# A factorization-machine layer on one core: the product of the squares as eight block products of three passes each, and another order of the first products

## The chip, the core and the metric

The kernel runs on one core of one Trainium2 chip. The core's engines run side by side, each with its own queue of instructions: TensorE (PE; its weight loads are listed as PEld), VectorE (DVE), ScalarE (ACT), GpSimd (POOL), and SyncE (SP), which here only starts transfers. DMAs are started from the queues of SP, ACT and POOL; those of POOL can add what they bring to what lies at the destination. The metric is the device time of one execution in microseconds.

## The reference

x is 1024 x 512, weight 64 x 512 x 512 (e, f, m), lin_w 512 x 512, all float32:

```python
out_lin = x @ lin_w.T + lin_b
xv = jnp.einsum('bf,efm->bem', x, weight)
zp = jnp.einsum('bf,efm->bem', jnp.square(x), jnp.square(weight))
interaction = 0.5 * jnp.sum(jnp.square(xv) - zp, axis=1)
return out_lin + interaction
```

The sum over e of zp is one product, of x squared with the sum over e of weight squared. It is 512 x 512 x 1024, as large as the linear one; the 64 products of xv are the bulk.

## The kernel before

All products are made by one level of Strassen's scheme: X (A11, A12, A21, A22: halves of the batch by halves of f) and the other operand are cut in four blocks, and seven products of sums of blocks take the place of eight. Everything is transposed so that f lies on the partitions, 128 at a time, two tiles (KH = 2) to half of f.

There are three stages.

1. **The linear stage**: seven products (`one_level`, line 504), each 4 matmuls of plain float32, 128 x 128 by 512. A plain float32 matmul appears in the profile as two instructions. The result waits in DRAM (`lin_dram`).
2. **The main stage**: 32 groups h of 512 columns (8 columns m for all 64 e), each with the products 1, 6, 2, 3, 7, 5, 4 in that order (`ORDER`), where product 5 is made a group ahead. A product is two halves; a half is two 128-row tiles j, held by one of four double banks of PSUM (`banks`). Each operand is split into float32r parts H, L and K (`split` for weights, `x_pieces` for X, once), and a half is made by three passes: front (H and L, 8 matmul instructions in a half) and back (K, 4 in a half), where the back passes come later by `LAG` slots, and between the two the bank is scaled and added to (DVE, or ACT for product 5). The loads of w11, w12, w21, w22 land in rings of raw tiles; T is their running sum, made by adding DMAs (`load`, `load_more`): T = w11 + w12 for product 5, + w22 for 6, + w21 for 4. `split` makes H on ACT and L on POOL or DVE, and K on POOL. `finish` squares a finished bank on ACT into a ring of two tiles, and DVE sums over e into `acc`. `w_squares` squares a raw weight tile and sums over e into `w2_sum`. In group 0, products 1 and 2 (`PLAIN`) are plain float32. Product 5 of group 0 comes first of all.
3. **The last stage**, the product of the squares: X is loaded again and squared, Strassen's sums of the squares are made by adding DMAs (`add_square`), those of `w2_sum` on POOL (`column_sums`), and `one_level` makes the seven products, plain float32 again. Each half of a sum is added to the output tiles as it comes (`into`, 128 x 512), and these are stored. The output tiles hold the linear result from DRAM and, by an adding DMA, the accumulator (`acc_dram`, written by `turn`, which transposes 32 columns at a time). The last quarter of the accumulator's columns comes by a load of its own (`last`) and a DVE operation.

The order of all this is not written out. Each operation is entered with `plan.add` and its cost in us on the engines that can do it; `key` gives PE's order, and `Plan.order` lays out the others by due times in a list schedule over 60 rounds, which it improves where PE waited in its own reckoning. What it gives is a fixed order for each engine. Costs it reckons with are `PASS` = 0.2267 for a float32r matmul instruction and `WHOLE` = 0.858 for a plain matmul; a DMA takes 1.6 us of the wire (3.1 if it adds) and 2.5 us to land. `both=True` marks DVE operations that the planner keeps apart from POOL's.

Buffers go by rings, and many of the last stage's tiles lie in rings of the main stage: X's squares in raw tiles, output tiles in the tiles kept for products 1 and 5. `home` and `give_back` do the same for the linear stage's tiles at the start.

Names in the profile leave out numbers: `w` is any tile of the rings w11 to w22 or the kept tile w, `p` those kept for products 1 and 5 (and at the start what lies there), `sq` and `wsq` squares, `pH`, `pL`, `pK` the weight's parts, `X1H` to `X7K` X's parts. Lines of helpers: 360 ACT's, 366 and 372 DVE's two kinds, 378 POOL's, 385 the sums over e, 392 plain DMAs, 397 adding ones; 697 is the main stage's matmul, 522 that of `one_level`, 511 that of its first product.

Of the kernel before, what the change touches and what calls it, by code (L numbers as in the profile page):

```python
# [18 lines left out]
P = 128  # L19
# [3 lines left out]

PE, DVE, ACT, POOL, SP = "PE", "DVE", "ACT", "POOL", "SP"

PLAIN = (1, 2)
LAG = 4
ORDER = (1, 6, 2, 3, 7, 5, 4)
SPLIT = {**dict.fromkeys(range(1, 8), POOL), 2: DVE, 3: DVE}
MORE = True  # L30
X_SPLIT = {5: DVE, 6: DVE, 3: DVE, 7: DVE, 1: DVE, 2: "DMA", 4: "DMA"}
FIRST = dict.fromkeys(range(1, 8), POOL)
SCALE = {1: "DVE", 5: "ACT"}
RAW = {"w11": 2, "w12": 2, "w21": 1, "w22": 2, "T": 2}
PIECES = {"H": 3, "L": 3, "K": 3}
# [6 lines left out]
class Plan:  # L42
# [104 lines left out]
    def forward(self, chain):  # L147
# [62 lines left out]
        while len(done) < len(ops):  # L210
            now = heapq.heappop(times)
            moved = True
            while moved:
                moved = False
                for e in pending:
# [7 lines left out]
                        continue  # L223
                    moved = True
                    if e == PE:
                        nxt, mark = nxt + 1, running[PE]
                        late = max(late, now - o.latest)
                    cost = o.costs[e]
                    o.start, o.engine = now, e
# [27 lines left out]
def kernel(  # L257
# [118 lines left out]
    def pool(o, a, b, sub, reads, writes, size=1024):  # L376
        def emit(_):
            return (nc.gpsimd.tensor_sub if sub else nc.gpsimd.tensor_add)(o, a, b)  # L378

        plan.add({POOL: 0.1 + 2.24 * size / 1024}, emit, reads, writes)  # L380
# [14 lines left out]
    def dma_add(o, i, reads, writes, move=3.1, land=2.5):  # L395
        plan.add(
            {POOL: 0.62}, lambda _: nc.gpsimd.dma_start(o, i, accum_op=ALU.add),  # L397
            tuple(reads) + tuple(writes), writes, land=land, move=move,
        )

    def used(*names):
        plan.add({NONE: 0.0}, None, (), names)
# [98 lines left out]
    def four():  # L501
        return [both_of(banks()) for _ in range(4)]
# [101 lines left out]
    def src(h, q):  # L604
        return weight[h // NCB, q][:, h % NCB]

    def load(h, n, q):
        now[h, n] = raw[n]()
        dma(buf[now[h, n]], src(h, q), (), (now[h, n],))

    def load_more(h, n, q):

        o = now[h, n]
        if h or MORE:
            dma_add(buf[o], src(h, q), (), (o,))
        else:
            i = now[h, QUAD[q]]
            pool(buf[o], buf[o], buf[i], False, (o, i), (o,))

    def w_squares(h, q):  # L620
        row, col = divmod(QUAD.index(q), 2)
# [20 lines left out]

    def prepare(h, p):
        if p == 5:
            load(h, "T", 0)
            if h:
                load_more(h, "T", 1)
                load(h, "w11", 0)
            load(h, "w12", 1)
            if not h:  # L650
                load_more(h, "T", 1)
                load(h, "w11", 0)
                load(h, "w22", 3)
                load(h, "w21", 2)
            w_squares(h, "w12")
        if p == 1:
            if h:
                load(h, "w22", 3)
            w_squares(h, "w11")
        if p == 6:  # L660
            load_more(h, "T", 3)
            if h:
                load(h, "w21", 2)
            w_squares(h, "w22")
        if p == 2:
            w_squares(h, "w21")
        if p == 7:
            load_more(h, "w12", 3)
        if p == 4:
            load_more(h, "T", 2)  # L670
        n = now[h, RHS[p]]
        return n if not h and p in PLAIN else split(n, SPLIT[p] if h else FIRST[p])

# [95 lines left out]

    for g in range(NG):  # L770
        acc_name[g] = acc_ring()
    product(0, 5)
    for h in range(NH):
        for p in ORDER:
            if p != 5:
                product(h, p)
            elif h + 1 < NH:
                product(h + 1, p)
            if not h:
                give_back(*(n for n in ("A11", "A12", "A22") if OPERAND[p] == n))  # L780
        if h % NCB == NCB - 1 and h + 1 < NH:
            turn(h // NCB)
# [1 line left out]


    out_dst = out.rearrange("(c p) b -> p c b", p=P)
    sq_home = {}
    for n, q in (("A21", "T"), ("A22", "w11"), ("A11", "w22"), ("A12", "w12")):
        sq_home[n] = raw[q]()
    for n, q in (("R5", "w11"), ("R6", "w21"), ("R3", "w12")):  # L790
        sq_home[n] = raw[q]()
    sq_home["R7"] = sq_home["A21"]

    def load_square(n, again=None):
        r, q = quads[n]
        o = sq_home[n]
        dma(buf[o], x_src[:, ts(q, KH), ts(r, H)], (), (o,))
        if again:
            act(buf[sq_home[again]], buf[o], AF.Square, (o,), (sq_home[again],))
        act(buf[o], buf[o], AF.Square, (o,), (o,))  # L800

    def add_square(n, m):
        o, i = sq_home[n], sq_home[m]
        dma_add(buf[o], buf[i], (i,), (o,))

    def minus(n, m):
        o, i = sq_home[n], sq_home[m]
        act(buf[o], buf[i], AF.Copy, (i,), (o,), scale=-1.0)

    load_square("A21")  # L810
    minus("A21", "A21")
    load_square("A22", "R5")
    add_square("R5", "A21")
    load_square("A11", "R6")
    add_square("R6", "R5")
    add_square("R7", "A11")
    load_square("A12")
    minus("R3", "A12")
    add_square("R3", "R6")
    w2 = {(r, c): w2_sum[:, ts(r, KH), ts(c, HM)] for r in range(2) for c in range(2)}  # L820
    w2_names = {z: (("w2h", *z),) for z in w2}
    for (r, c), ap in w2.items():
        plan.add({ACT: 0.6}, lambda _, ap=ap: nc.scalar.mul(ap, ap, -0.5),
                 tuple(("w2", r, m) for m in range(M)
                       if ("w2", r, m) in plan.writer and m // HM == c), w2_names[r, c])
    wt_home = [raw[q]() for q in ("w22", "T")]
    wt = {
        k: buf[wt_home[(k - 1) // 2]][:, (k - 1) % 2].rearrange("p (k m) -> p k m", k=KH)
        for k in range(1, 5)
    }  # L830
    wt_names = {k: (("wt", k),) for k in range(1, 5)}
    for z, n in enumerate(wt_home):
        used(n, ("wt", 2 * z + 1), ("wt", 2 * z + 2))
    column_sums(w2, wt, w2_names, wt_names,
                lambda o, a, b, r, w: pool(o, a, b, False, r, w, 512))
    act(wt[2], wt[2], AF.Copy, wt_names[2], wt_names[2], 512, -1.0)
    left = {i: (buf[sq_home[n]], (sq_home[n],)) for i, n in OPERAND.items()}
    right = rhs_of(w2, w2_names, wt, wt_names)

    turn(NG - 1)  # L840
    o_name = {}

    def acc_names(ch):
        return tuple(("accd", g, q) for g in range(NG) for q in range(P // MG)
                     if g * MG // P == ch)

    for (r, c), n in (((0, 0), "p1"), ((1, 0), "p1"), ((1, 1), "p5"), ((0, 1), "p5")):
        n = o_name[r, c] = kept[n]()
        for u in range(2):
            used((n, u), n)  # L850
        dma(buf[n], lin_dram[:, ts(c, 2), ts(r, H)], (("lind", r, c),), both_of(n))
        for u in range(2):
            ch = 2 * c + u
            if ch < M // P - 1:
                dma_add(buf[n, u], acc_dram[:, ch, ts(r, H)], acc_names(ch), ((n, u),), 1.4, 5.0)

    def into(n, bank, sub, u):
        o = buf[n][:, u]
        dve(o, o, buf[bank[u]], sub, ((n, u), bank[u]), ((n, u),))

    def store(r, c, u):
        n = o_name[r, c]
        dma(out_dst[:, 2 * c + u, ts(r, H)], buf[n, u], ((n, u),), (), 1.0, (SP, ACT))

    def columns(n, m, sub, u):
        o, i = buf[n][:, u], buf[m][:, u]
        dve(o, o, i, sub, ((n, u), (m, u)), ((n, u),), 512, True)

    v, f2, f5, f4 = four()
    f3 = f4[0], f2[0]  # L870
    key = slot[0]
    one_level(1, right, left, v, True, key)
    one_level(2, right, left, f2, True, key + 4)
    for u in range(2):
        into(o_name[0, 0], v, False, u)
        into(o_name[0, 0], f2, False, u)
        store(0, 0, u)
    one_level(5, right, left, f5, True, key + 6)
    z = kept["w"]()
    for u in range(2):  # L880
        used((z, u), z)
        act(buf[z, u], buf[f5[u]], AF.Copy, (f5[u],), ((z, u),), 512)
        for r in range(2):
            columns(o_name[r, 1], z, True, u)
    one_level(6, right, left, v, False, key + 8)
    for u in range(2):
        into(o_name[0, 1], v, True, u)
    one_level(4, right, left, f5, True, key + 11)
    for u in range(2):
        into(o_name[1, 0], f5, False, u)  # L890
    last = wsquare()
    for r in range(2):
        used((last, r), last)
    for r in (1, 0):
        dma(buf[last][:, r], acc_dram[:, M // P - 1, ts(r, H)], acc_names(M // P - 1),
            ((last, r),), 1.0)
        n = o_name[r, 1]
        stt(buf[n, 1], buf[last][:, r], 0.5, buf[n, 1], ALU.add, ((last, r), (n, 1)), ((n, 1),),
            512, True)

    one_level(7, right, left, v, False, key + 14)
    for u in range(2):
        into(o_name[1, 1], v, True, u)
        store(1, 1, u)
        into(o_name[1, 0], v, False, u)
        store(1, 0, u)
    one_level(3, right, left, f3, True, key + 17)
    for u in range(2):
        into(o_name[0, 1], f3, True, u)
        store(0, 1, u)  # L910

    for op, engine in plan.order():
        if op.emit:
# [40 lines left out]
```

## Time and profile before

| | us |
|---|---|
| runs, median of 3 (lowest to highest) | 1285.91 (1285.85 to 1286.28) |
| the profiled execution, its own time | 1285.96 |
| its span, first to last instruction | 1284.0 |

The granted clock of TensorE was 0.999 of full speed over the span. HBM was read for 160.43 MB and written for 6.29 MB, 130 GB/s over the span.

How rows are read. A row of groups has: line, engine, operation, out<-in by names, shapes, xcount, then busy time, mean ns of one, and the idle time of the engine before them with what ended it. A row of the timeline has the start and the length in us, then the same, with idle time before it and its releaser in brackets. A row of waits has who waited for whom: us in total, times, longest. The chain that ended last has start, length and what. DMA rows have KB of one and the median us from issue to landing.

### The profile page before, as it was taken

The numbers are of one execution on the slowest core, as the hardware profiler recorded it, in microseconds if no ns is written. First come the engines' busy times: TensorE is split into PE (matmuls) and PEld (weight loads), VectorE is DVE, ScalarE is ACT, GpSimd is POOL, SyncE is SP. The second block draws the span as 40 slices with busy tenths as digits, with TensorE's granted clock in tenths as the row PEclk, the third lists the DMA queues.
The fourth block names the chain that finished last, engine by engine and source line by source line (L and its number), as shares of the span: only waits on it lengthen the run. The fifth ranks groups of instructions, "written<-read, shape, count | busy, mean of one in ns | idle before, by whom it ended". The sixth has DMA issues, their size and how long they took to land.

```text
span 1284.0 us, 15422 instructions
## 1 busy us (share of the span) xinstructions
PE 1277.9 (100%) x5476; PEld 1024.1 (80%) x5476; DVE 1224.3 (95%) x1018; ACT 963.9 (75%) x1005; POOL 1043.5 (81%) x532
## 2 busy tenths in 40 slices
PE   9999999999999999999999999999999999999998
PEld 4688888888888888888888888888888888888883
DVE  7799999999999999999999999999999999999996
ACT  6677877777787777877777878777778777787781
POOL 2888898888898888898888888888889878889881
PEclk9999999999999999999999999999999999999999
DMA  8966654446654445664445664444665435665456
GB/s 237 210 175 148 148 118 123 101 108 151 148 129 123 99 110 139 152 142 118 108 102 130 148 152 115 120 98 114 152 148 128 120 85 122 145 152 131 126 112 168
DMA packets 68077, 171.93 MB, mean 134 GB/s; under 512 B 22944, under 2 KB 23968, under 8 KB 68000
## 3 DMA queue, kind: packets, MB, share of 16 engines
q0 software_dynamic: 20448, 72.89, 33.4%
q1 hardware_dynamic: 45296, 94.91, 22.1%
q10 hardware_dynamic: 2256, 3.15, 0.7%
q8 instruction: 43, 0.70, 0.2%
q14 instruction: 34, 0.28, 0.1%
HBM read 160.43 MB, written 6.29 MB: 130 GB/s over the span
## 4 chain that ended last, share of the span: by engine, by line
PE 94%; DVE 3%; DMA 2%; ACT 0%; issue 0%; ACTq 0%; SPq 0%; DVEq 0%
PE bank L697 92%; PE bank L522 2%; DMA w<-weight 1%; DMA p<-lin_wT 1%; DVE pL L366 0%; DVE bank L366 0%; DVE acc L385 0%; DVE X3K L366 0%; DVE p L372 0%; DVE w L372 0%; ACT pH L360 0%; ACT sq L360 0%; ACTq L427 0%; DVE X7K L366 0%; DVE sq L366 0%
## 5 line engine op out<-in xcount | busy, mean ns | idle before, releaser
L378 POOL TENSOR_TENSOR pK<-pH,pL 128x1024 fp32r<-128x1024 f32 x222 | 570.8, 2574 | 161.9 <-PE bank L697 157.5
L360 ACT ACTIVATE sq<-bank 128x1024 f32<-128x1024 f32 x256 | 261.9, 1024 | 93.8 <-issue 48.5
L385 DVE TENSOR_REDUCE acc<-sq 128x16 f32<-128x1024 f32 x256 | 308.5, 1205 | 1.3 <-ACT sq L360 1.2
L378 POOL TENSOR_TENSOR pL<-T,pL 128x1024 fp32r<-128x1024 f32 x96 | 256.7, 2674 | 12.9 <-ACT pH L360 10.7
L366 DVE SCALAR_TENSOR_TENSOR bank<-bank,w 128x1024 f32<-128x1024 f32 x192 | 233.8, 1218 | 0.7 <-PE bank L697 0.6
L372 DVE TENSOR_TENSOR w<-bank,p 128x1024 f32<-128x1024 f32 x128 | 155.6, 1216 | 26.8 <-PE bank L697 26.7
L360 ACT ACTIVATE p<-bank 128x1024 f32<-128x1024 f32 x128 | 131.0, 1023 | 59.9 <-PE bank L697 59.4
L366 DVE SCALAR_TENSOR_TENSOR pL<-pH,w 128x1024 fp32r<-128x1024 f32 x62 | 167.4, 2700 | 0.0
L366 DVE SCALAR_TENSOR_TENSOR bank<-bank,p 128x1024 f32<-128x1024 f32 x128 | 153.0, 1216 | 5.4 <-ACT p L360 4.5
L360 ACT ACTIVATE pL<-T 128x1024 fp32r<-128x1024 f32 x96 | 101.1, 1054 | 75.5 <-issue 68.3
L385 DVE TENSOR_REDUCE w_sum<-wsq 128x16 f32<-128x1024 f32 x128 | 154.1, 1204 | 2.5 <-ACT wsq L360 2.5
L378 POOL TENSOR_TENSOR pL<-w,pL 128x1024 fp32r<-128x1024 f32 x64 | 154.4, 2412 | 0.4 <-issue 0.4
L360 ACT ACTIVATE pH<-w 128x1024 fp32r<-128x1024 f32 x126 | 133.0, 1056 | 11.9 <-PE bank L697 10.3
L360 ACT ACTIVATE wsq<-w 128x1024 f32<-128x1024 f32 x128 | 134.6, 1052 | 0.4 <-DVE w_sum L385 0.4
L397 POOL DMA_DIRECT2D T<-weight x96 | 92.5, 963 | 36.7 <-POOL pL L378 17.5
L360 ACT ACTIVATE pH<-T 128x1024 fp32r<-128x1024 f32 x96 | 101.2, 1054 | 0.0
L360 ACT ACTIVATE pL<-w 128x1024 fp32r<-128x1024 f32 x64 | 67.9, 1061 | 43.6 <-PE bank L697 25.0
L697 PE MATMUL bank<-pH,X4H 128*128 128x512 f32 x256 | 81.4, 399 | 0.0
L697 PE MATMUL bank<-pH,X6H 128*128 128x512 f32 x256 | 78.9, 389 | 0.3 <-ACT p L360 0.3
L697 PE MATMUL bank<-pH,X5H 128*128 128x512 f32 x256 | 79.2, 391 | 0.0
L697 PE MATMUL bank<-pL,X4L 128*128 128x512 f32 x256 | 79.1, 390 | 0.0
L697 PE MATMUL bank<-pH,X3H 128*128 128x512 f32 x256 | 78.9, 390 | 0.1
(114 smaller groups left out, 2545.8 us busy)
## 6 DMA issues: line engine op xcount, KB each, us to landing
w<-weight SPq DMA_DIRECT2D x128, 512.0 KB, 5.8
T<-weight POOLq DMA_DIRECT2D x96, 512.0 KB, 6.1
T<-weight SPq DMA_DIRECT2D x32, 512.0 KB, 4.8
w<-weight POOLq DMA_DIRECT2D x32, 512.0 KB, 6.8
accd<-turned SPq DMA_DIRECT2D x64, 32.0 KB, 5.8
p<-lind SPq DMA_DIRECT2D x4, 512.0 KB, 4.5
out<-p ACTq DMA_DIRECT2D x8, 256.0 KB, 2.5
w<-xT SPq DMA_DIRECT2D x6, 256.0 KB, 4.9
```

Source lines behind the costliest of these rows:

```text
L360: nc.scalar.activation(o, i, func, bias=bias, scale=scale)
L366: return nc.vector.scalar_tensor_tensor(o, i, scalar, j, ALU.mult, op)
L372: return (nc.vector.tensor_sub if sub else nc.vector.tensor_add)(o, a, b)
L378: return (nc.gpsimd.tensor_sub if sub else nc.gpsimd.tensor_add)(o, a, b)
L385: lambda _: nc.vector.tensor_reduce(o, i.rearrange("p a (m e) -> p a m e", e=E), axis=AX.X, op=ALU.add),
L397: {POOL: 0.62}, lambda _: nc.gpsimd.dma_start(o, i, accum_op=ALU.add),
L522: made = nc.tensor.matmul(buf[bank[u]], b[:, k, ts(u, P)], a[:, k, :], start=first and k == 0, stop=k == KH - 1, skip_group_check=True,)
L697: made = nc.tensor.matmul(buf[bank, j], buf[x][:, k, ts(2 * half + j, P)], buf[w][:, k, :], start=first and k == 0, stop=k == KH - 1, skip ...
```

## The change

- The last stage has no Strassen sums. `w2_sum` times -0.5 is split into parts H, L, K for each half r of f (`sums`), in tiles of X5's and X1's parts: the upper half with L and K by adding DMAs, the lower by DVE. The four squared blocks of X are split likewise (`squares`) into tiles of X6's, X2's and X3's parts and one set of the weight's; L is made on POOL for A11 and A12, by an adding DMA for A21 and A22, and K on POOL.
- `passes` makes each of four output blocks (r, c) by 16 front and 8 back matmul instructions of float32r; `into` adds a whole double bank (128 x 1024) to the output tile with a scale on DVE, `into_half` half of one for the last.
- In group 0, product 2 is no longer plain. Product 1 comes first and 5 behind it. T isn't loaded: T = w11 + w12 and T + w22 are DVE sums of loaded tiles (`sum_of`). Product 5's L in group 0 is made by DVE. The last addition to T, and group 1's T, stay adding DMAs.
- In the planner, an order set between PE and an early transfer hangs on the last PE operation that emits something.

```diff
-PLAIN = (1, 2)
+PLAIN = (1,)
-MORE = True
+SUMS = {0: "DMA", 1: DVE}
+SQUARES = {"A11": POOL, "A12": POOL, "A21": "DMA", "A22": "DMA"}
-FIRST = dict.fromkeys(range(1, 8), POOL)
+FIRST = {**dict.fromkeys(range(1, 8), POOL), 5: DVE}
...
-                        nxt, mark = nxt + 1, running[PE]
+                        nxt += 1
+                        if running[PE] and running[PE].emit:
+                            mark = running[PE]
...
+    def sum_of(n, a, b):
+
+        o, a, b = raw[n](), now[0, a], now[0, b]
+        now[0, n] = o
+        dve(buf[o], buf[a], buf[b], False, (a, b), (o,), 1024, True)
...
         if p == 5:
-            load(h, "T", 0)
             if h:
+                load(h, "T", 0)
                 load_more(h, "T", 1)
                 load(h, "w11", 0)
-            load(h, "w12", 1)
-            if not h:
-                load_more(h, "T", 1)
-                load(h, "w11", 0)
-                load(h, "w22", 3)
-                load(h, "w21", 2)
+                load(h, "w12", 1)
+            else:
+                sum_of("T", "w11", "w12")
             w_squares(h, "w12")
         if p == 1:
             if h:
                 load(h, "w22", 3)
+            else:
+                for q in (0, 1, 3, 2):
+                    load(h, QUAD[q], q)
             w_squares(h, "w11")
         if p == 6:
-            load_more(h, "T", 3)
             if h:
+                load_more(h, "T", 3)
                 load(h, "w21", 2)
+            else:
+                sum_of("T", "T", "w22")
...
-    product(0, 5)
     for h in range(NH):
         for p in ORDER:
...
+            if not h and p == 1:
+                product(h, 5)
...
+    squares, sums = {}, {}
+    for r, pieces in enumerate((("X5H", "X5L", "X5K"), ("X1H", "X1L", "X1K"))):
+        w2 = w2_sum[:, ts(r, KH)]
+        names = tuple(("w2", r, m) for m in range(M) if ("w2", r, m) in plan.writer)
+        sums[r] = h, l, k = pieces
+        act(buf[h], w2, AF.Copy, names, (h,), scale=-0.5 * TRIM)
+        if SUMS[r] == DVE:
+            stt(buf[l], w2, -0.5, f32(h), ALU.subtract, (h, *names), (l,), 1024, True)
+            stt(buf[k], f32(h), -U, f32(l), ALU.add, (h, l), (k,), 1024, True)
+        else:
+            half = (("w2h", r),)
+            act(w2, w2, AF.Copy, names, names + half, scale=-0.5)
+            act(buf[l], w2, AF.Copy, half, (l,), scale=-TRIM)
+            dma_add(f32(l), w2, half, (l,))
+            act(buf[k], w2, AF.Copy, half, (k,), scale=-U * TRIM)
+            dma_add(f32(k), f32(l), (l,), (k,))
+    for n, q, pieces in (
+        ("A11", "T", ("X6H", "X6L", "X6K")), ("A12", "w11", ("X2H", "X2L", "X2K")),
+        ("A21", "w22", ("X3H", "X3L", "X3K")), ("A22", "w12", [piece[z]() for z in "HLK"]),
+    ):
+        (r, z), o = quads[n], raw[q]()
+        dma(buf[o], x_src[:, ts(z, KH), ts(r, H)], (), (o,))
         act(buf[o], buf[o], AF.Square, (o,), (o,))
+        squares[r, z] = h, l, k = pieces
+        act(buf[h], buf[o], AF.Copy, (o,), (h,), scale=U * TRIM)
+        if SQUARES[n] == POOL:
+            act(buf[l], buf[o], AF.Copy, (o,), (l,), scale=TRIM)
+            pool(buf[l], buf[o], f32(l), True, (o, l), (l,))
+        else:
+            act(buf[l], buf[o], AF.Copy, (o,), (l,), scale=-TRIM)
+            dma_add(f32(l), buf[o], (o,), (l,))
+        pool(buf[k], f32(h), f32(l), True, (h, l), (k,))
...
+    BLOCKS = (0, 0), (1, 0), (0, 1), (1, 1)
+    for (r, c), n in zip(BLOCKS, ("p1", "p1", "p5", "p5")):
...
+    def into(n, bank, scale):
+        stt(buf[n], buf[bank[0][0]], scale, buf[n], ALU.add, (*bank, *both_of(n)), both_of(n), 1024)
...
+    def passes(which, r, c, bank, key):
+        for u in range(2):
+            for z in range(2):
+                def emit(_, u=u, z=z):
+                    for i in which:
+                        for k in range(KH):
+                            w, x = buf[sums[z][i]], buf[squares[r, z][i]]
+                            made = nc.tensor.matmul(
+                                buf[bank[u]], w[:, k, (2 * c + u) * P:(2 * c + u + 1) * P],
+                                x[:, k, :], start=z == 0 and i == which[0] and k == 0,
+                                stop=z == 1 and i == which[-1] and k == KH - 1,
+                                skip_group_check=True,
+                            )
+                    return made
...
+    b = four()
+    key = slot[0]
+    for at, (r, c) in enumerate(BLOCKS):
+        n = o_name[r, c]
+        front, back = b[2 * at % 4], b[(2 * at + 1) % 4]
+        passes((0, 1), r, c, front, key + 6 * at)
+        if at < 3:
+            into(n, front, S + 1.0)
+        if c == 1:
+            dma(buf[last][:, r], acc_dram[:, M // P - 1, ts(r, H)], acc_names(M // P - 1),
+                ((last, r),), 1.0)
+            stt(buf[n, 1], buf[last][:, r], 0.5, buf[n, 1], ALU.add, ((last, r), (n, 1)),
+                ((n, 1),), 512, True)
+        if at < 3:
+            passes((2,), r, c, back, key + 6 * at + 4)
+            into(n, back, S)
+        else:
+            into(n, front, S + 1.0)
+            back = back[0], b[0][1]
+            passes((2,), r, c, back, key + 6 * at + 4)
+            for u in range(2):
+                into_half(n, back, S, u)
+        for u in range(2):
+            store(r, c, u)
```

The lines that this replaces (`load_square`, `add_square`, `minus`, the uses of `column_sums` and `one_level`, `columns`) stand in the kernel above.

More of the change, by code (lines that the diff above doesn't have):

```diff
@@ L613, in load_more @@
         o = now[h, n]
[L614 to L618, printed above, removed]
+        dma_add(buf[o], src(h, q), (), (o,))
+    def sum_of(n, a, b):
+        o, a, b = raw[n](), now[0, a], now[0, b]
+        now[0, n] = o
+        dve(buf[o], buf[a], buf[b], False, (a, b), (o,), 1024, True)
     def w_squares(h, q):
@@ L786 @@
     out_dst = out.rearrange("(c p) b -> p c b", p=P)
[L787 to L799, printed above, removed]
-        act(buf[o], buf[o], AF.Square, (o,), (o,))
@@ L802, in add_square @@
[L802 to L838, printed above, removed]
+    squares, sums = {}, {}
[14 more added lines that the diff above has]
+            dma_add(f32(k), f32(l), (l,), (k,))
@@ L840 @@
     turn(NG - 1)
-    o_name = {}
     def acc_names(ch):
@@ L845, in acc_names @@
                      if g * MG // P == ch)
-    for (r, c), n in (((0, 0), "p1"), ((1, 0), "p1"), ((1, 1), "p5"), ((0, 1), "p5")):
+    o_name = {}
+    BLOCKS = (0, 0), (1, 0), (0, 1), (1, 1)
+    for (r, c), n in zip(BLOCKS, ("p1", "p1", "p5", "p5")):
         n = o_name[r, c] = kept[n]()
@@ L855, with into_half @@
                 dma_add(buf[n, u], acc_dram[:, ch, ts(r, H)], acc_names(ch), ((n, u),), 1.4, 5.0)
-    def into(n, bank, sub, u):
-        o = buf[n][:, u]
-        dve(o, o, buf[bank[u]], sub, ((n, u), bank[u]), ((n, u),))
+    def into(n, bank, scale):
+        stt(buf[n], buf[bank[0][0]], scale, buf[n], ALU.add, (*bank, *both_of(n)), both_of(n), 1024)
+    def into_half(n, bank, scale, u):
+        o = buf[n, u]
+        stt(o, buf[bank[u]], scale, o, ALU.add, (bank[u], (n, u)), ((n, u),))
     def store(r, c, u):
@@ L863, in store @@
         dma(out_dst[:, 2 * c + u, ts(r, H)], buf[n, u], ((n, u),), (), 1.0, (SP, ACT))
[L865 to L890, printed above, removed]
+    def passes(which, r, c, bank, key):
[12 more added lines that the diff above has]
+                    return made
+                reads = [t[i] for i in which for t in (sums[z], squares[r, z])]
+                plan.add({PE: len(which) * KH * PASS}, emit, (*reads, bank[u]), (bank[u],),
+                         key=key + 0.2 * u + 0.1 * z)
     last = wsquare()
@@ L893 @@
         used((last, r), last)
[L894 to L910, printed above, removed]
+    b = four()
[22 more added lines that the diff above has]
+            store(r, c, u)
     for op, engine in plan.order():
```

## The prediction

> **What bounds the kernel now.** I read the page's head and engine totals first, then what TensorE (PE) waited for, then the end of the chain that ended last.
>
> ```profile
> span 1284.0 us, 15422 instructions
> PE 1277.9 (100%) x5476; PEld 1024.1 (80%) x5476; DVE 1224.3 (95%) x1018; ACT 963.9 (75%) x1005; POOL 1043.5 (81%) x532
> ```
>
> ```profile
> PE bank L539 <- PEq L943: 0.8, 1, 0.8
> PE bank L522 <- issue: 0.6, 1, 0.6
> PE bank L697 <- ACT p L360: 0.3, 1, 0.3
> ```
>
> PE is busy in all but 6 us of the span, and its three waits sum to 1.7 us; the rest of the 6 us is the tail behind its last matmul. A matmul's busy time is modelled, so the spacing of starts is the price used below, not the busy share. DVE stands at 95%, which matters as soon as something is added to it.
>
> ```profile
> 1083.69 169.28 PE bank L697 x744
> 1252.96 3.43 PE bank L522 x8
> 1256.40 1.85 PE bank L697 x8
> 1258.24 13.73 PE bank L522 x32
> 1271.98 0.59 issue
> 1272.57 7.12 PE bank L522 x16
> 1279.71 0.69 DVE p L372
> ```
>
> This end of the chain shows the stage that is rewritten: 56 instructions of line 522 (8 + 32 + 16) with the last product's eight back passes between, one wait of 0.59 us, and one DVE add, after which the last store takes 1284.0 - 1280.4 = 3.6 us. So the time is PE's work, plus its waits, plus a tail. A change counts where it alters one of the three.
>
> **PE's work.** Two prices are needed: a pass (a matmul instruction on float32r parts) and an instruction of a plain float32 matmul.
>
> ```profile
> 45.82 3.59 PE L697 MATMUL bank<-w,w 128*128 128x512 f32 x8
> 48.85 1.48 PE L697 MATMUL bank<-pK,X6K 128*128 128x512 f32 x4
> 50.17 3.60 PE L697 MATMUL bank<-w,w 128*128 128x512 f32 x8
> 53.20 1.48 PE L697 MATMUL bank<-pK,X6K 128*128 128x512 f32 x4
> 54.53 0.62 PE L697 MATMUL bank<-pH,X3H 128*128 128x512 f32 x2
> ...
> 1241.92 0.61 PE L697 MATMUL bank<-pH,X7H 128*128 128x512 f32 x2
> ...
> 1244.64 0.61 PE L697 MATMUL bank<-pH,X7H 128*128 128x512 f32 x2
> ...
> 1261.51 7.03 PE L522 MATMUL bank<-w,w 128*128 128x512 f32 x16
> 1268.38 3.60 PE L522 MATMUL bank<-w,T 128*128 128x512 f32 x8
> ```
>
> Half a product, 12 passes, takes 1244.64 - 1241.92 = 2.72 us: 0.2267 us a pass. Sixteen plain instructions take 1268.38 - 1261.51 = 6.87 us: 0.4294 us each, two to a matmul. The last stage now is 28 matmuls, 56 x 0.4294 = 24.05 us. The new one is four blocks of 24 passes, 96 x 0.2267 = 21.76 us: **-2.29 us**. Eight products instead of seven cost less because three passes (0.680) are cheaper than one plain matmul (0.859). The first group's product 2 leaves plain float32: its rows above give 54.53 - 45.82 = 8.71 us less eight passes, 6.90 us (16 x 0.4294 = 6.87); as 24 passes it is 5.44 us: **-1.43 us**. Product 1 stays plain, the linear stage is untouched. Together -3.72 us. The trace has no pass with w2_sum's parts as the stationary tile; its bounds are 0.2267 (all shapes are those of line 697) and, far above it, half a plain matmul, 0.4294. I take the first, since shape and type are the same; break-even is 24.05/96 = 0.2505.
>
> The Trainium skill, "FP8 and Floating Point Precision", section TensorE Precision Notes, has true FP32 as four passes through the array. By that 28 plain matmuls would be 112 passes, 25.39 us, and product 2 would be 32, 7.25 us, so the two edits would bring -3.63 and -1.81. The trace has 0.859 for a matmul against 4 x 0.2267 = 0.907, so the smaller gain stands.
>
> **The start.** Product 1 moves ahead of product 5, whose operand T becomes a DVE sum of two loaded tiles.
>
> ```profile
> 26.29 2.35 POOL L378 TENSOR_TENSOR pL<-T,pL 128x1024 fp32r<-128x1024 f32 x1 [10.70 <-ACT pH L360]
> ...
> 28.95 0.89 POOL L397 DMA_DIRECT2D T<-weight  x1 [0.31 <-POOL pL L378]
> ...
> 52.45 1.88 POOL L397 DMA_DIRECT2D X2L<-w  x1
> ...
> 61.88 0.87 POOL L397 DMA_DIRECT2D X2K<-X2L  x1
> ```
>
> Now pL for T is done at 28.64 us, and the first product starts at 28.78: a margin of 0.14. Then product 1 will need only w11 (a load, 5.8 us in the rows below) and X's block, and product 5 starts 6.87 us later, at 35.65. Removed: the load of T and two adding DMAs for group 0 (the rows at 28.95 and an earlier one). Added: two DVE sums and, for product 5, a DVE split in place of POOL's. Two instructions of one kind bound them: 1.22 us free, 2.70 us where POOL holds it up (rows below), so 3.7 to 8.1 us on DVE; I take 5. They lie beside product 1's 6.87 us. Without that cover they would cost up to 1.2 us.
>
> Product 2's split adds 2 ACT copies and 5 us of POOL. X2's parts move: they land after 61.88 + 10.0 now, and are wanted at 28.78 + 6.87 + 2 x 5.44 = 46.5 (L) and 7.25 later (K). The two adds move ahead of POOL's splits, 0.9 to 1.9 us of its queue each; the splits behind them gain from POOL's 10.70 us of idling. I cost this at nothing; planned just in time it could cost 2 to 4 (a rival).
>
> The wait of 0.3 us, at 43.9, is for an ACT copy that stood behind a split waiting for an adding DMA. With the order changed I count it as gone; it may come back.
>
> **The end, beside PE.** PE's stage begins at 1252.80 now, and so at 1252.80 - 1.43 - 0.33 = 1251.04. It runs front of block 0 (3.63 us), the last product's eight passes (1.81), then the rest: PE ends at 1251.04 + 1.81 + 21.76 = 1274.6.
>
> ```profile
> L366 DVE SCALAR_TENSOR_TENSOR bank<-bank,w 128x1024 f32<-128x1024 f32 x192 | 233.8, 1218 | 0.7 <-PE bank L697 0.6
> L366 DVE SCALAR_TENSOR_TENSOR pL<-pH,w 128x1024 fp32r<-128x1024 f32 x62 | 167.4, 2700 | 0.0
> ```
>
> ```profile
> 1240.00:1250.00 10.00, 10.00 (x46) 8.29 (x45) 9.99 (x10) 6.86 (x8) 10.00 (x9) 1.00 0.52 92
> 1250.00:1260.00 10.00, 10.00 (x35) 6.20 (x34) 9.65 (x10) 4.62 (x5) 5.30 (x6) 1.00 1.07 180
> ```
>
> The second fence gives, per stretch, busy us of PE, weight loads, DVE, ACT and POOL, clock, and DMA share. ACT gets 17 copies and squares at about 1.05 us for some 12.8 us of its own before: +5, and it idles 3.1 + 5.4 us here. POOL gets two L and four K at 2.4 us for four sums (8.7 us): +5.7, and four adding DMAs as before; it is busy for 5.30 of the second ten and for little behind them. DVE loses twenty half adds (20 x 0.68 = 13.6) and gets seven whole ones and four halves (7 x 1.22 + 4 x 0.68 = 11.3) plus the two part splits of w2_sum's lower half (2.4 to 5.4): 0 to +3 us. These two lie before or just after the stage's start, where DVE is full. The banks are the tight place:
>
> ```profile
> 1250.28 1.23 DVE L372 TENSOR_TENSOR w<-bank,p 128x1024 f32<-128x1024 f32 x1 [0.29 <-PE bank L697]
> ...
> 1263.67 0.45 DVE L760 STREAM_TRANSPOSE turned<-acc 128x256 f32<-128x256 f32 x1 [2.82 <-DMA accd<-turned]
> ...
> 1270.39 0.69 DVE L372 TENSOR_TENSOR p<-p,w 128x512 f32<-128x512 f32 x1 [2.13 <-DMA p<-accd]
> ...
> 1272.98 0.68 DVE L366 SCALAR_TENSOR_TENSOR p<-wsq,p 128x512 f32<-128x512 f32 x1
> ```
>
> ```profile
> 1251.60 1.03 ACT L360 ACTIVATE sq<-bank 128x1024 f32<-128x1024 f32 x1 [0.41 <-DVE w L372]
> ```
>
> The bank of the stage's first sum is free when this square ends, 1252.63, and used at 1252.80: a margin of 0.17 that the change keeps. A late DVE is therefore a late PE. I take 0.3 us for this (bounds 0 and 2.4, one POOL operation in the way).
>
> The wait of 0.59 goes: its bank was read by a DVE add queued behind the one that waited 2.13 us for p<-accd. In the new order a bank is written again only a block and a half after it was read. What is late next is the last channel's accumulator: transposed at 1263.67, stored, loaded, added at 1272.98. All of that moves by 1.76 us, to 1271.2. DVE then has a half (0.60), a whole (1.14), a half and a whole before the last two halves: 1271.2 + 3.48 + 0.60 + 0.68 = 1276.0. Bounded by PE alone DVE would end at 1274.6 + 0.2 + 0.68 = 1275.5. I take 1275.9, near the first, as that chain is all of measured steps; the store's 3.6 follows.
>
> **The sum.** Span 1275.9 + 3.6 = 1279.5, less certain by the 0.3 above: 1279.8. The profiled execution took 1285.96 us, 1.96 more than its span, and the median of the runs is 1285.91, the same within 0.05. So 1279.8 + 1.96 = **1281.8 us**.
>
> **The rivals.** The adding DMAs set the prices of two of them:
>
> ```profile
> w<-weight SPq DMA_DIRECT2D x128, 512.0 KB, 5.8
> ...
> X2L<-w POOLq DMA_DIRECT2D x1, 512.0 KB, 8.4
> ...
> X2K<-X2L POOLq DMA_DIRECT2D x1, 512.0 KB, 10.0
> ...
> T<-w POOLq DMA_DIRECT2D x1, 512.0 KB, 9.8
> ```
>
> ```profile
> 1231.52 1.21 DVE L385 TENSOR_REDUCE w_sum<-wsq 128x16 f32<-128x1024 f32 x1
> ```
>
> *Slower: w2_sum's upper half comes too late.* Its L and K are two adding DMAs one behind the other; the planner prices each at 0.62 + 3.1 + 2.5 = 6.2 us, the rows at up to 9.8 and 10.0. L is wanted at the stage's start S, K at S + 5.44. Issued as late as the planner's price allows, at S - 7.0, L lands at S + 2.8, and K 10.0 later at S + 12.8, wanted then at S + 8.2: 2.8 + 4.6 = 7.4 us on 1281.5, 1288.9 us. Against it: the upper half's last reduce ends at 1232.73, 20.1 before the stage's start now, and with three ACT copies and both landings K is there at 1232.73 + 3.2 + 19.8 = 1255.7, ahead of 1252.80 + 5.44 = 1258.2 (times of before, both of which move alike). It decides once that reduce, or POOL's place for the add, slips by more than 2.5 us, and makes the kernel slower from about 9.5.
>
> *DVE takes the place.* One of w2_sum's splits meets a POOL operation when the first bank should be freed: 2.4 us, 1283.9. For it: DVE's 9.99 of 10 us and the 2.70 against 1.22. Against: part of DVE's work in this stretch, sums of the accumulator, can stand back. The Trainium skill, "SBUF — State Buffer", Who interferes with whom, says that a DVE operation with two SBUF inputs and a GpSimd operation that reads SBUF shut each other out for a whole instruction; the two rows agree with that (2.70 against 1.22).
>
> *X2's parts late at the start.* An add that lands 2.2 to 3.8 us behind its planned 6.2: 1284.0 to 1285.6. Against: POOL idles 10.70 us before 26.29, and X's blocks are there by then.
>
> *The last accumulator later still*, by 2.5 us more behind DMAs (share 1.07 in the row above): 1284.3, as a longer tail.
>
> *The passes don't keep 0.2267*: at 0.2505 the stage gains nothing, 1281.8 + 2.3 = 1284.1.
>
> **How the numbers follow.** Forecast 0.62 (1280.8 to 1283.0), DVE 0.14, X2 0.06, the accumulator 0.06, passes 0.04, slower 0.08. A measurement of this kernel can tell about 0.2% from no change, 2.6 us: faster is below 1283.3, slower above 1288.5. Faster gets the forecast, half of the DVE case and a few hundredths of the other small ones, 0.73; slower 0.08; the rest, 0.19, lies between. The range goes from 1280.6 (no waits, DVE bound by PE, 0.5 us of luck in the tail) up to 1286.0, which takes in all but the slower case and a little of the others.
>
> **What would show it.** In the changed profile: no line of 522 behind the linear stage; 96 instructions of a new matmul line at 0.2267 from start to start; product 2's first group as passes; PE's first product from w11 at about 28.8 with product 5 at 35.7; the last PE start near 1274.4; the end of the chain with at most two DVE adds. It is wrong if PE waits over 1.5 us in all behind the first microsecond, if the last DVE operation stands more than 1.5 us behind PE's end, or if the passes are spaced wider.

## The result, and the profile after

The changed kernel takes 1295.39 us (median of 6 runs, 1294.74 to 1296.04), the kernel before 1286.10 us (6 runs): ratio 1.0072, 95% interval 1.0062 to 1.0082. It is slower by 9.3 us, where 1281.8 was forecast.

The head of the page after, and PE's one wait behind the first microsecond:

```profile
span 1294.2 us, 15587 instructions
PE 1276.7 (99%) x5524; PEld 1035.6 (80%) x5524; DVE 1243.5 (96%) x1014; ACT 966.6 (75%) x1008; POOL 1055.9 (82%) x533
```

```profile
PE bank L864 <- ACT sq L363: 12.1, 1, 12.1
```

The two small waits of before are gone, and one of 12.1 us stands at the first matmul of the new last stage (line 864). The chain that ended last says what is behind the ACT square that ended it:

```profile
1246.89 13.78 DVE X1K L369
1260.68 1.15 DVE w L375
...
1261.91 1.03 ACT sq L363
...
1262.98 6.70 PE bank L864 x16
```

One DVE operation, X1K (K of w2_sum's lower half), lasts 13.8 us. Behind it on DVE's queue stands the subtraction `w`, then ACT's square, and these two free the bank that PE wants. The same operation in DVE's timeline, and below it what POOL did meanwhile (start, length):

```profile
1246.81 13.87 DVE L369 SCALAR_TENSOR_TENSOR X1K<-X1H,X1L 128x1024 fp32r<-128x1024 f32 x1
1260.60 1.21 DVE L375 TENSOR_TENSOR w<-bank,p 128x1024 f32<-128x1024 f32 x1
```

```profile
1245.09 3.38 POOL L381 TENSOR_TENSOR pK<-pH,pL 128x1024 fp32r<-128x1024 f32 x1
1247.44 1.87 POOL L400 DMA_DIRECT2D pL<-w  x1
1248.03 2.19 POOL L400 DMA_DIRECT2D p<-accd  x1
1248.59 4.00 POOL L381 TENSOR_TENSOR X6K<-X6H,X6L 128x1024 fp32r<-128x1024 f32 x1
1250.94 3.94 POOL L381 TENSOR_TENSOR X2K<-X2H,X2L 128x1024 fp32r<-128x1024 f32 x1
1253.22 3.40 POOL L400 DMA_DIRECT2D p<-accd  x2
1254.37 4.62 POOL L381 TENSOR_TENSOR X3K<-X3H,X3L 128x1024 fp32r<-128x1024 f32 x1
1256.65 3.17 POOL L400 DMA_DIRECT2D p<-accd  x1
1257.26 5.61 POOL L381 TENSOR_TENSOR pK<-pH,pL 128x1024 fp32r<-128x1024 f32 x1
```

POOL has no idle time in any of these rows (there would be a bracket). They overlap: X2K starts 2.35 us behind X6K, so in a length of 4 us and more POOL is in part still at the operation before. X1K came while the first pK ran, and ended at 1260.68: 1.7 us behind the end of X3K (1258.99) and 2.2 us ahead of that of the last pK (1262.87). The wait also costs behind itself. PE's rows at the stage's start and the same pass later, and two stretches (busy us of PE, weight loads, DVE, ACT, POOL, then clock, DMA share and GB/s):

```profile
1249.78 1.07 PE L704 MATMUL bank<-pK,X7K 128*128 128x512 f32 x4
1262.98 1.22 PE L864 MATMUL bank<-X6H,X5H 128*128 128x512 f32 x2 [12.13 <-ACT sq L363]
...
1269.52 2.00 PE L704 MATMUL bank<-pK,X4K 128*128 128x512 f32 x8
...
1278.61 0.62 PE L864 MATMUL bank<-X6H,X5H 128*128 128x512 f32 x2
1279.06 0.62 PE L864 MATMUL bank<-X6L,X5L 128*128 128x512 f32 x2
```

```profile
1250.00:1260.00 10.00, 0.85 (x4) 0.38 (x2) 10.00 (x1) 0.00 (x0) 10.00 (x8) 0.76 0.95 165
1260.00:1270.00 10.00, 7.01 (x19) 5.55 (x20) 8.68 (x8) 2.05 (x2) 3.75 (x2) 0.55 0.53 107
```

The granted clock falls to 0.55 in the ten us after 1260, and the first 16 passes take 1269.52 - 1262.98 = 6.54 us instead of 16 x 0.2267 = 3.63; the same passes of block 2 take 0.45 us for two (1278.61 to 1279.06). So the wait costs 12.1 + 2.9 = 15.0 us. Without it the span would be 1294.2 - 15.0 = 1279.2 us, against the 1279.8 of the forecast's sum.

From span to span: +10.2 us. Up to the point where the last stage could begin -2.1 (1249.78 + 4 x 0.2267 = 1250.69, where before it began at 1252.80), the wait and its surroundings +12.3, the stage itself -0.2 (-2.3 of work and -0.6 of a wait, +2.9 of the low clock, +-0.2 by the rows' ends), and the tail +0.2. The ends of PE's last rows divide stage and tail, 1279.68 before and 1289.65 after.

### The profile page after: what moved, and what is told of

It is laid out like the page before. It is cut to its first block, busy times and chain, and to the rows that moved or that the text cites. A ratio compares the mean times of both kernels' runs of the same rounds, so it can differ in the third digit from the quotient of the medians.

```text
span 1294.2 us, 15587 instructions
## 1 busy us (share of the span) xinstructions
PE 1276.7 (99%) x5524; PEld 1035.6 (80%) x5524; DVE 1243.5 (96%) x1014; ACT 966.6 (75%) x1008; POOL 1055.9 (82%) x533
## 4 chain that ended last, share of the span: by engine, by line
PE 97%; DVE 2%; ACT 1%; issue 0%; DVEq 0%; ACTq 0%
PE bank L704 93%; PE bank L864 2%; PE bank L525 1%; DVE X1K L369 1%; PE bank L514 1%; PE bank L542 0%; DVE bank L369 0%; DVE acc L388 0%; ACT sq L363 0%; DVE p L369 0%; DVE w L375 0%; DVE X1L L369 0%; ACT pL L363 0%; ACT pH L363 0%; ACT X6L L363 0%
## 5 line engine op out<-in xcount | busy, mean ns | idle before, releaser
L381 POOL TENSOR_TENSOR pK<-pH,pL 128x1024 fp32r<-128x1024 f32 x224 | 594.3, 2653 | 176.5 <-PE bank L704 167.1
L381 POOL TENSOR_TENSOR pL<-T,pL 128x1024 fp32r<-128x1024 f32 x95 | 238.4, 2510 | 0.6 <-ACT pL L363 0.6
L381 POOL TENSOR_TENSOR pL<-w,pL 128x1024 fp32r<-128x1024 f32 x65 | 175.2, 2696 | 0.0
L400 POOL DMA_DIRECT2D T<-weight x94 | 83.5, 981 | 11.5 <-POOL pL L381 9.0
L704 PE MATMUL bank<-pL,X5L 128*128 128x512 f32 x256 | 78.8, 389 | 0.0
L704 PE MATMUL bank<-pL,X2L 128*128 128x512 f32 x256 | 78.8, 389 | 0.0
```

Of the source, the lines that this page charges most:

```text
L704: made = nc.tensor.matmul(buf[bank, j], buf[x][:, k, ts(2 * half + j, P)], buf[w][:, k, :], start=first and k == 0, stop=k == KH - 1, skip ...
```

## The experiments

The theory after these profiles: an operation of DVE with two inputs in SBUF and a tensor operation of POOL shut each other out (what they share is called the port below). DVE was kept out of the port as long as POOL had its next tensor operation at hand, since none of POOL's operations waited for X1K, and a bank hung on the operation behind it. The main rival: the last stage gives DVE, POOL and ACT more than they can do beside PE, so that something is late in any order. Six of the kernels take the order of the changed kernel on every engine, and only move one operation in it or add waits.

The edits of these six stand at the end, where the planner's list is emitted. `op.writes` holds the names that an operation writes, `at` finds the last operation that writes a name, and `after` names one operation of another engine that this one waits for. Dots mark what is left out.

### X1K earlier, and X6K waits for it

```diff
-    for op, engine in plan.order():
+    done = plan.order()
+    at = {op.writes[0]: i for i, (op, _) in enumerate(done) if op.writes and op.emit}
+    k = done.pop(at["X1K"])
+    done.insert(at["X1L"] + 1, k)
...
+    done[at["X6K"]][0].after = k[0]
+    for op, engine in done:
```

> Edit: on DVE, X1K (the second split of w2_sum's lower half) stands directly behind X1L, two operations earlier, beside three DMA issues of POOL; POOL's X6K waits for it. Theory (DVE was kept out of the port that it shares with POOL, by a run of POOL operations without a pause): X1K takes 1.2 to 2.5 us instead of 13.87, the wait of 12.13 us at the last stage's start and the half clock behind it (some 2.9 us) go: 1280.4 to 1282 us. Rival (the last stage has too much work beside PE: ACT, POOL and DVE are late whatever the order): a wait of over 5 us stays, 1287 us or more.

Measured: 1286.54 us (10 runs, 1284.2 to 1288.72), ratio to the kernel before 1.0007 (0.9997 to 1.0017). The long wait is gone, but the time is 4.5 us above what was expected and within 0.5 us of the rival's. X1K and the operation before it on DVE, two rows of POOL, and PE's waits:

```profile
1243.34 1.22 DVE L369 SCALAR_TENSOR_TENSOR X1L<-w_sum,X1H 128x1024 fp32r<-128x1024 f32 x1
1244.58 4.93 DVE L369 SCALAR_TENSOR_TENSOR X1K<-X1H,X1L 128x1024 fp32r<-128x1024 f32 x1
```

```profile
1244.52 1.49 POOL L400 DMA_DIRECT2D X3L<-w  x1
1245.08 3.34 POOL L381 TENSOR_TENSOR pK<-pH,pL 128x1024 fp32r<-128x1024 f32 x1
```

```profile
PE bank L864 <- ACT sq L363: 2.2, 1, 2.2
...
PE bank L704 <- DVE bank L369: 0.8, 1, 0.8
```

X1K came while POOL was issuing DMAs, and was kept out all the same, until the pK behind them had ended (1248.4; X1K ends at 1249.5). The three operations now behind it were late, PE waited 0.8 and 2.2 us, and the first eight passes ran at half pace. X1L, which also has two inputs in SBUF, came in the same run of three DMA issues with the same pK behind them, 1.74 us ahead of pK's row, and took 1.22 us; X1K came 0.50 us ahead of it. So here the DMA issues left the port to the operation that came early among them, and not to the one that came late. How early is enough, these rows don't show.

### X6K waits for X1K, nothing is moved

```diff
...
+    done[at["X6K"]][0].after = done[at["X1K"]][0]
...
```

> Edit: the order of the changed kernel, but POOL's X6K waits for DVE's X1K. Theory: X1K gets in behind POOL's pK and two DMA issues and ends between 1249.6 and 1251.3; w and the square follow, PE starts its last stage 1.1 to 2.9 us late, at full clock: 1281.5 to 1283.4 us. Rival (too much work): 1287 us or more, the more as POOL is held up.

Measured: 1282.03 us in a single run. The same kernel was then run six times:

> The kernel whose X6K waits for X1K, with no other edit, timed. Theory: as in its one look, a wait of 1 us at the last stage's start: 1282.0 us, within 1 us, ratio 0.997; against the changed kernel 13 us faster by one wait of one POOL operation. Rival (the one look was luck): 1285 us or more.

1282.43 us (6 runs, 1281.92 to 1283.19), ratio to the kernel before 0.9972 (0.9961 to 0.9983). The timelines of DVE, POOL and PE in the single run:

```profile
1246.78 2.71 DVE L369 SCALAR_TENSOR_TENSOR X1K<-X1H,X1L 128x1024 fp32r<-128x1024 f32 x1
```

```profile
1245.06 3.34 POOL L381 TENSOR_TENSOR pK<-pH,pL 128x1024 fp32r<-128x1024 f32 x1
1247.42 1.82 POOL L400 DMA_DIRECT2D pL<-w  x1
1248.00 2.13 POOL L400 DMA_DIRECT2D p<-accd  x1
1249.58 2.97 POOL L381 TENSOR_TENSOR X6K<-X6H,X6L 128x1024 fp32r<-128x1024 f32 x1
```

```profile
1251.80 0.73 PE L864 MATMUL bank<-X6H,X5H 128*128 128x512 f32 x2 [0.97 <-ACT sq L363]
```

X1K starts where it started in the changed kernel, beside the same pK and the same two DMA issues, and ends at 1249.49, 1.1 us behind pK's end: it got in at once, beside the DMA issues. The one difference is that the tensor operation behind them was not free to run. X6K itself ends at 1252.55 with the wait and at 1252.59 without it, so POOL lost nothing by it. One wait of one POOL operation is worth 1295.4 - 1282.4 = 13 us.

### X2K waits for X1K, one operation later

```diff
...
+    done[at["X2K"]][0].after = done[at["X1K"]][0]
...
```

> Edit: as before, but the first POOL operation that waits for X1K is X2K, one later than X6K. Theory: X1K ends one POOL operation later, near 1253.7; PE's last stage starts some 5.2 us late, and part of it runs at half clock (0 to 3 us): 1285.6 to 1288.6 us. Rival (DVE gets in by itself between any two POOL operations): no different from the kernel whose X6K waits.

Measured: 1287.92 us in a single run. X1K (min, median and max of its length in ns, from first to last start) and PE's wait:

```profile
L369 DVE SCALAR_TENSOR_TENSOR X1K<-X1H,X1L x1: 6829/6829/6829, 1247.1 to 1247.1; 128x1024 fp32r<-128x1024 f32 x1
```

```profile
PE bank L864 <- ACT sq L363: 5.1, 1, 5.1
```

As expected: X1K ends at 1247.1 + 6.8 = 1253.9, one POOL operation later, and PE waits 5.1 us. DVE doesn't get in by itself between pK and X6K.

### X1K behind everything that frees a bank, no POOL operation waits

```diff
...
+    last = max(i for i, (op, _) in enumerate(done)
+               if op.costs.keys() == {DVE} and op.writes[0] == ("bank_3", 0) and op.latest < done[at["X3K"]][0].latest)
+    done.insert(last + 1, done[at["X1K"]])
+    done.pop(at["X1K"])
...
```

> Edit: no POOL operation waits; X1K stands five operations later on DVE, behind the scaling of the last product's second bank. Theory: X1K is shut out as before until POOL waits for something else (1259 to 1260.7), but nothing that frees a bank stands behind it: PE starts its last stage on time and waits at the first pass that reads X1K, 3 to 4.5 us: 1283.5 to 1285.5 us. Rival (too much work): the same lateness as in the changed kernel, 1293 to 1296 us.

Measured: 1288.74 us in a single run, 3 us above what was expected, and below the rival's. X1K on DVE, and PE's waits:

```profile
1255.22 6.85 DVE L369 SCALAR_TENSOR_TENSOR X1K<-X1H,X1L 128x1024 fp32r<-128x1024 f32 x1
```

```profile
PE bank L864 <- DVE X1K L369: 4.2, 1, 4.2
PE bank L514 <- DMA p<-lin_wT: 0.9, 1, 0.9
PE bank L542 <- PEq L941: 0.8, 1, 0.8
PE bank L525 <- DVE p L375: 0.6, 1, 0.6
```

The last stage starts with no wait, and PE stops at the first pass that reads X1K, which is shut out for 5.6 us again (6.85 less the 1.22 that it takes alone). The 4.2 us were foreseen. Not foreseen were 1.5 us of waits at the first load of lin_w, which nothing in the edit touches, and a clock of 0.51 from 1260 to 1265 us, about the end of the stop. So both halves of the theory hold by themselves: the exclusion, and what hangs behind the excluded operation.

### X1K behind the subtraction, and X6K waits

```diff
...
+    i, k = at["w_0"], done.pop(at["X1K"])
+    done.insert(i, k)
...
+    done[at["X6K"]][0].after = k[0]
```

> Edit: on DVE, X1K stands one operation later, behind the subtraction that frees the last stage's first bank, and POOL's X6K waits for it. Theory (DVE kept out of the port, and a bank behind it): X1K gets in at once, as POOL stands still, about 1.2 us; PE starts the last stage on time, no wait over 0.5 us there: 1280.5 to 1281.8 us, ratio 0.996 to 0.997. Rival (holding POOL back makes its parts late): a wait of 1 us or more at a pass that reads X6K, X2K or X3K, 1282 to 1284 us.

Measured: 1282.08 us (6 runs, 1281.81 to 1283.27), ratio 0.9968 (0.9956 to 0.9980). The ratio is as expected; the time is 0.3 us above the theory's and just inside the rival's, though no wait of 1 us at such a pass appears. X1K takes 1.22 us, and the stage starts on time; the 1 us that this saves is partly given back, since X3K and the last K come later and PE waits 0.5 us for POOL:

```profile
1250.83 1.22 DVE L369 SCALAR_TENSOR_TENSOR X1K<-X1H,X1L 128x1024 fp32r<-128x1024 f32 x1
```

```profile
PE bank L864 <- POOL pK L381: 0.5, 1, 0.5
```

It can't be told from the kernel with X6K's wait alone: 1282.08 against 1282.43, with intervals of 0.1% each way. Both beat the kernel before and the changed one.

### A wait wherever the planner took the port for free

```diff
...
+    guard = None
+    for op, engine in done:
+        if engine == DVE and op.both:
+            guard = op
+        elif engine == POOL and not op.move and guard is not None:
+            if op.after is None:
+                op.after = guard
+            guard = None
...
```

> Edit: in the changed kernel's order, wherever a DVE operation that the planner marks as needing the shared port isn't yet waited for, the next POOL tensor operation waits for it (nine places, X6K behind X1K among them). Theory: as with X6K's wait alone, X1K in under 3 us and a wait of about 1 us at the last stage's start: 1281.5 to 1283 us, ratio 0.997. Rival (holding POOL up at more places costs): a wait of over 2 us, 1283.5 us or more.

Measured: 1282.51 us (8 runs), ratio 0.9971 (0.9961 to 0.9981); PE's one wait at the last stage's start is 1.0 us, X1K takes 2.73. The general rule costs no more than the one wait.

### The lower half by adding DMAs

```diff
-SUMS = {0: "DMA", 1: DVE}
+SUMS = {0: "DMA", 1: "DMA"}
```

> Edit: w2_sum's lower half is split by adding DMAs like the upper one, so that DVE makes neither X1L nor X1K; the planner lays out the order anew. Theory (the port): no wait of over 3 us at the last stage's start, since no DVE operation there needs the port; the two added DMAs one behind the other may come late by 0 to 3 us: 1281 to 1285 us. Rival (too much work at the end, whoever does it): 1288 us or more.

Measured: 1285.41 us (10 runs, 1283.86 to 1287.81), ratio 0.9994 (0.9984 to 1.0005); the profiled execution took 1283.86. That is the fastest of the ten. PE has no wait at the stage's start, and one of 1.3 us later in the stage, behind a DVE addition:

```profile
PE bank L864 <- DVE p L369: 1.3, 1, 1.3
```

Without DVE's two splits the long wait doesn't arise, in an order that the planner made anew, though POOL has as much to do. The median lies 0.4 us above what was expected, and no gain over the kernel before can be told; what the other nine executions lose isn't shown.

### Each half of the change alone

The new start with the old last stage (the code from `out_dst` up to the planner's loop is the old one):

> The changed order of the first products (product 1 ahead, T by DVE sums, product 2 as passes) with the old last stage. Prediction's term: -1.43 us of PE work and up to -0.3 of a wait: ratio 0.9985 to 0.9990, 1284.0 to 1284.6 us where the kernel before takes 1285.9. Rival (the start gives its gain back in waits): no wait fewer and a ratio of 1.000.

Measured: 1284.86 us (10 runs, 1282.77 to 1285.57), ratio 0.9981 (0.9971 to 0.9991). PE has no wait but the first:

```profile
PE bank L542 <- PEq L951: 0.8, 1, 0.8
```

The gain is 1.2 to 3.7 us by the interval, somewhat more than was expected (ratio 0.9985 to 0.9990), while the time itself lies 0.3 us above the range expected. The -1.43 of work and both waits of before, 0.33 and 0.59, are gone, which sums to 2.35.

The old start with the new last stage:

> The old start with the new last stage, in the order that the planner makes of that. In this order POOL's X6K and the last product's K wait for a DVE operation, and X1K stands behind everything on DVE that frees a bank. Theory: no long wait: -2.29 us of PE work and the wait of 0.6 gone, 1282.5 to 1284 us, ratio 0.9975 to 0.9985. Rival (the new last stage is slow in any order): a wait of over 5 us, 1288 us or more.

Measured: 1290.56 us (4 runs, 1289.63 to 1293.1), ratio 1.0037 (1.0024 to 1.0051). This misses what was expected, though there is no long wait: PE waits 1.2 us for X1K, 0.7 and 0.5 elsewhere in the stage. The end is set by something else, in DVE's timeline and PE's last row. (The execution shown is the slowest of the four, 2.5 us above their median.)

```profile
1281.38 0.69 DVE L368 SCALAR_TENSOR_TENSOR p<-wsq,p 128x512 f32<-128x512 f32 x1 [4.02 <-DMA wsq<-accd]
...
1284.02 2.42 DVE L368 SCALAR_TENSOR_TENSOR p<-bank,p 128x1024 f32<-128x1024 f32 x3
```

```profile
1279.88 0.61 PE L858 MATMUL bank<-pK,X1K 128*128 128x512 f32 x2
```

PE is done at 1280.3, DVE at 1286.4: five us behind what PE alone would allow (1280.3 + 0.2 + 0.7). The last accumulator came late, its stores 7.2 us in landing by the chain, and what was left of the adds of two blocks stood behind it on DVE. That is the prediction's rival of the last accumulator, in another order than the changed kernel's, at twice its price.

## Why the prediction was wrong

**PE's work: right.** The sum's largest term, -3.72 us, stands: 96 passes at 0.2267 from start to start where the clock is full (1278.61 to 1279.06 for two), and product 2 as passes. Both waits of before are gone. The start was right in its order and times:

```profile
29.34 7.03 PE L704 MATMUL bank<-w,w 128*128 128x512 f32 x16
35.80 1.03 PE L704 MATMUL bank<-pH,X5H 128*128 128x512 f32 x2
```

Product 1 and product 5 begin at 29.3 and 35.8 (forecast 28.8 and 35.7), the two DVE sums and product 5's split take 1.22 us each (the lower of the bounds; they stand at 19.1 to 23.8, ahead of product 1 and not beside it), and X2's adds are issued at 12.9 and 20.0, so nothing waits for them.

**What failed is one step**: "I take 0.3 us for this (bounds 0 and 2.4, one POOL operation in the way)", and with it the 2.4 us of the DVE rival and the range's upper end. The mechanism was named as a rival, its place too (DVE held up at the port when the first bank should be freed); its size was 12.1 us of wait and 2.9 of low clock, six times the bound. The bound came from the row of 62 `pL` operations, mean 2.70. In the trace before, the longest of them took 4.12 us, already 2.9 us over the 1.22 that it takes alone (shortest, median, longest in ns):

```profile
L366 DVE SCALAR_TENSOR_TENSOR pL<-pH,w x62: 1215/2442/4125, 76.2 to 1227.5; 128x1024 fp32r<-128x1024 f32 x62
```

Those are another case: `split` has POOL make K from that same L, so that this K waits for DVE by its data. In the trace before, at most one tensor operation of POOL begins within any of the 62, and the first that begins behind each is a `pK`. X1K is read by PE alone. Nothing on POOL waits for it, and POOL's next operations were at hand for 12 us. Giving X6K that wait brought X1K to 2.71 us, the mean of that row, and the kernel to 1282.4, within 0.6 us of the forecast.

The planner's reckoning missed the same thing: its `both` operation was to fit beside DMA issues of POOL, and it ordered no POOL operation behind it.

The Trainium skill, "SBUF — State Buffer", Summary: rules for kernel authors, says that of two such operations the second to issue is blocked until the first finishes. Here it stayed blocked through three more tensor operations that began later than it (13.87 us). The two rows that the prediction set beside this page (2.70 against 1.22) fit both cases and couldn't tell the one from the other.

**The other rivals.** W2_sum's upper half was in time: with X6K's wait no pass waits for X5L or X5K. The passes kept their pace. The last accumulator wasn't late in the changed kernel, where DVE's last adds wait 1.7 us for PE, and it was late in the old start with the new stage.

**What stays open**: why DVE, waiting since 1246.8, didn't get in when pK ended at 1248.47, with two DMA issues before POOL's next tensor operation, while it did with that operation held back. The runs show that it is so (13.87 against 2.71 us), not by what rule the port is given. It is open too why DVE got in ahead of the end of the last pK: the landing that this pK needs (A22's L, 7.7 us after an issue at 1247.44 to 1249.31) was there when pK's row begins at 1257.26, so a tensor operation was at hand then as well. In the kernel with X1K behind everything that frees a bank, X1K got in ahead of the last pK too (ends at 1262.07 and 1264.29).

## What to carry to other kernels

The price of one DVE operation with two inputs in SBUF ran here from 1.22 to 13.87 us, with what POOL had queued and which of POOL's operations waited for it. Don't take it as bounded by one POOL operation: check who reads its result, and give POOL's next tensor operation a wait where only another engine does. A mean from the same kind of instruction holds only where the same operations wait on each other. And see what stands behind such an operation on its own queue: here a 1.2 us operation whose result PE reads only in the K passes held up the one that frees the bank that PE needed next.

## What the runs showed of the hardware

DMA issues of POOL were not in DVE's way by themselves (X1K got in beside two of them, X1L beside three). An operation that came when only 0.50 us of them were left ahead of a queued tensor operation was kept out until that one had ended (4.93 us in the first experiment).

PE's clock fell after short waits. A wait of 1.0 us left it at 1.00 (X6K's wait alone). Waits of 0.8 and 2.2 us with four passes between them (the first experiment) brought the mean of ten us to 0.83, and the passes behind them were spaced some 0.43 us at first:

```profile
1254.08 1.22 PE L864 MATMUL bank<-X6H,X5H 128*128 128x512 f32 x2 [2.18 <-ACT sq L363]
1255.10 1.05 PE L864 MATMUL bank<-X6L,X5L 128*128 128x512 f32 x2
...
1257.44 0.63 PE L864 MATMUL bank<-X6H,X5H 128*128 128x512 f32 x2
```

```profile
1250.00:1260.00 10.00, 7.11 (x24) 5.46 (x25) 9.77 (x9) 2.05 (x2) 10.00 (x8) 0.83 1.05 211
```

The eight passes from 1254.08 to 1257.44 took 3.36 us instead of 8 x 0.2267 = 1.81, so the two waits, 3.0 us together, cost another 1.5. A wait on PE had two prices here, its own length and that of the clock.
